# Cross-attention with image prompts: the context transposed by VectorE instead of TensorE, with its load and a few stages around it moved

## The chip, the cores and the metric

The kernel runs on one NeuronCore of a Trainium2 chip, all in fp32. Its engines are TensorE (PE; its weight loads are shown apart as PEld), VectorE (DVE), ScalarE (ACT), GpSimd (POOL) and SyncE (SP), which here only issues DMAs. The metric is the time of one execution on the device in microseconds, the median of several runs. Before the change it was 448.66 us (three runs, 448.07 to 451.15 us).

## The reference

Eight batches (B) of 112 queries with 320 channels attend, with 20 heads of 16 channels, to a context of 375 rows with 512 channels. The last 4 rows of each context are image prompts, the first 371 are text. Cut to what matters:

```python
q    = heads(x @ W_q);  k_t, v_t = heads(text @ W_k), heads(text @ W_v)
p    = softmax(q k_t^T / 4)                       # 112 x 371 per head
text_out = p v_t
qsem = l2norm(p @ text)                           # 112 x 512 per head
sem  = qsem @ l2norm(ip)^T                        # 112 x 4 per head
fused   = q k_ip^T / 4 + 0.5 * sem
probs_ip = softmax(fused) * spatial_mask
out  = (text_out + probs_ip v_ip) @ W_out + b_out + x
```

`p @ text` is never formed. Its norm is the root of p G p with the Gram matrix G = text text^T, and its product with the prompts comes from further columns that stand beside G.

## The kernel before, in words

**Tiling.** A batch has five groups of four heads. For a group, TensorE forms the scores of each head (`scores`, L592, tiles ps_s), VectorE takes the maximum of each row (`probabilities`, L605, nmx), ACT the exponential (L609, p) and a small copy of the prompt logits (L611, ipl), and SP sends p to a tile xg (L614). VectorE turns xg in squares of 32 (`transposed`, L622, xgT, 128 x 1536 elements). Then TensorE multiplies p by the batch's table u, which holds the Gram matrix, the prompts and the values (`multiplied`, L641, ps_qd: twelve steps of four heads side by side). ACT copies the last columns (`value_sums`, L654), and VectorE multiplies the others by p and sums them (`reduced`, L687, one instruction and one accumulator read per head). That frees the four PSUM banks of ps_qd for the next group.

**Between the groups.** After a group's multiplications, `between(b, g)` puts in a piece of other work. In groups 0 to 4 of batch b this is: `gram` of batch b+1 (L415); its `values` (L486); the rest of these and the first piece of its `keys` (L453); the second and third piece of the keys (L453, L444), and queries of later batches (L297, L305); and the transposed context of batch b+2 with further queries. The third piece of the keys is no product but three transposes of columns that were computed with the values. Beside these runs `finish` (called "f") of batch b−1, which joins text and prompts: its weights w (L771, VectorE) are followed on POOL by L827, L838, L839 and L840, which complete the tile attn in group 2 and 3; TensorE turns attn (ps_a, L845) in group 3 and multiplies by W_out (ps_o, L858) in group 4; VectorE adds the bias and residual (L818).

**The transposed context.** A load brings a context into a tile ct, rows on partitions: three DMAs of up to 128 rows of 2 KB and one for seven left-over rows (`load_ctx`, L129, L131). `transposed_context` turns it in three pieces: four TensorE transposes (L357) into one PSUM bank (ps_c) and one copy by ACT (L367) into ctxT, channels on partitions. Gram, values and keys read ctxT. POOL sets ctxT's last columns to zero (L331) and copies the normalised prompts into it (L410). Contexts 0 and 1 are turned in the prologue, the others in the loop.

**What sets the order.** PE, SP and DVE run in the order in which the program writes their instructions, in the main loop ACT too. POOL's order is left to a planner in the loop of the first seven batches, and only in the last batch is it written by hand. All waits come from the tiles' dependences. `run(key, make, pieces)` takes a generator a given number of pieces further. PSUM has eight banks: four for ps_qd, two for scores (`ps_sc`), two for the rest (`ps_mm`); `bank(name, spare=True)` takes one of the two score banks. Both pairs are handed out in turn, so a tile waits for whoever last used its slot. Each DMA queue's completion is counted on one of eight semaphores in turn; a DMA waits for the one issued eight before it.

Of the kernel before, what the change touches and what calls it, by code (L numbers as in the profile page):

```python
# [8 lines left out]
F32 = mybir.dt.float32  # L9
# [11 lines left out]
def kernel(  # L21
# [14 lines left out]
    nc = tc.nc  # L36
    P = 128
    B, S, C = x.shape
    T, E = ehs.shape[1:]
    H = HEADS  # L40
    D = C // H
    TT = T - NIP
    NT = (T + P - 1) // P
    TP = NT * P
    NE = E // P
# [3 lines left out]
    FULL = C // P  # L49
    REST = C - FULL * P  # L50
    RG = 32
# [4 lines left out]
    SCALE = D ** -0.5  # L56
    N = B * NIP

    GROUP = 4
    NG = H // GROUP  # L60
    BLK = TP // RG
    QN = P // RG
# [19 lines left out]
    def bank(name, spare=False):  # L82

        if spare:
            return ps_sc.tile([P, 512], F32, tag="sc", name=name)
        return ps_mm.tile([P, 512], F32, tag="mm", name=name)
# [25 lines left out]
        eng.dma_start(t[:REST, FULL, :C], w[FULL * P :, :])  # L112

    def load_embed(eng, t, w):
        eng.dma_start(t[:, :, :C], w.rearrange("(e p) f -> p e f", p=P))

    def spread(eng, t):

# [2 lines left out]
            eng.tensor_copy(v[:, :, a, 0, :], v[:, :, a // 2, a % 2, :])  # L121
        eng.memset(v[:, :, :, 1, :], 0.0)

    def load_ctx(b):
        ct = io.tile([P, NT, E], F32, tag="ct", name=f"ct_{b}")
        for c in range(NT):
            rows = min(P, T - c * P)
            some = rows - rows % 16
            nc.sync.dma_start(ct[:some, c, :], ehs[b, c * P : c * P + some, :])  # L129
            if some < rows:  # L130
                nc.sync.dma_start(ct[some:rows, c, :], ehs[b, c * P + some : c * P + rows, :])  # L131
        return ct
# [82 lines left out]
    def normalised_prompts():  # L215

        sq = work.tile([N, E], F32, tag="ipn", name="ipsq", bufs=1)
        ss = small.tile([N, 1], F32, tag="ipss", name="ipss", bufs=1)
        nc.vector.tensor_tensor_reduce(
            out=sq, in0=ip_sb, in1=ip_sb, scale=1.0, scalar=0.0, op0=ALU.mult, op1=ALU.add,  # L220
            accum_out=ss,
        )
        nc.vector.tensor_scalar_max(ss, ss, EPS * EPS)
        rn = small.tile([N, 1], F32, tag="iprn", name="iprn", bufs=1)
        nc.scalar.activation(rn, ss, AF.Sqrt)
        nc.vector.reciprocal(rn, rn)

        ipn = work.tile([N, E], F32, tag="ipn", name="ipn", bufs=1)
        nc.vector.tensor_scalar(ipn, ip_sb, rn, 0.5, op0=ALU.mult, op1=ALU.mult)
        yield  # L230

        for src, dst, n in ((ipn, ipnT, "n"), (ip_sb, ipT, "r")):
            ps = bank(f"ps_ipT{n}")
            for e in range(NE):
                nc.tensor.transpose(
                    ps[:, e * N : (e + 1) * N], src[:, e * P : (e + 1) * P], ident[:N, :N]
                )
            nc.vector.tensor_copy(
                dst, ps[:, : NE * N].rearrange("p (e n) -> p e n", n=N)
            )  # L240
        yield
# [82 lines left out]
    def load_next(b):  # L324
        if 2 <= b < B:
            loaded[b] = load_ctx(b)

    def begin(b):
        s = st[b] = dict(ct=loaded.pop(b))
        s["ctxT"] = work.tile([P, NE, TP], F32, tag="ctxT", name=f"ctxT_{b}")  # L330
        nc.gpsimd.memset(s["ctxT"][:, :, T:], 0.0)  # L331

        s["kT"] = work.tile([P, NC, T], F32, tag="kT", name=f"kT_{b}")
        s["vext"] = work.tile([P, NT, C + REST], F32, tag="vext", name=f"vext_{b}", bufs=1)
        s["k3"] = k3
        s["vd"] = dram.tile([TP, C], F32, tag="vd", name=f"vd_{b}")
        s["u"] = work.tile([P, UCOL], F32, tag="u", name=f"u_{b}")
        s["vr"] = work.tile([P, BLK, NG, D], F32, tag="vr", name=f"vr_{b}")
        s["ipl"] = work.tile([S, H, NIP], F32, tag="ipl", name=f"ipl_{b}")
        s["ss"] = work.tile([S, H], F32, tag="ss", name=f"ss_{b}")  # L340
        s["pvs"] = work.tile([S, H, VW], F32, tag="pvs", name=f"pvs_{b}")
        s["vip"] = work.tile([S, NIP, H, D], F32, tag="vipb", name=f"vip_{b}")
# [6 lines left out]
    def transposed_context(b):  # L349
        begin(b)  # L350
        s = st[b]
        ct, ctxT = s["ct"], s["ctxT"]
        for c in range(NT):
            rows = min(P, TT - c * P)
            ps = bank(f"ps_c_{b}_{c}", spare=b > 1 and c > 0)
            for e in range(NE):
                nc.tensor.transpose(  # L357
                    ps[:, e * P : e * P + rows],
                    ct[:rows, c, e * P : (e + 1) * P],
                    ident[:rows, :rows],  # L360
                )
            o = ctxT[:, :, c * P : c * P + rows]
            i = ps.rearrange("p (e t) -> p e t", t=P)[:, :, :rows]
            if c % 2 and b < 1:
                nc.vector.tensor_copy(o, i)
            else:
                nc.scalar.copy(o, i)  # L367
            yield
# [65 lines left out]
    def keys(b):  # L434
        s = st[b]
        if b > 0:
            nc.gpsimd.tensor_copy(s["kT"][:, :, TT:], kip[:, :, b * NIP : (b + 1) * NIP])
        for i in range(NC):
            ps = bank(f"ps_k_{b}_{i}")
            if 0 < b < B - 1 and i == FULL:  # L440

                for c in range(NT):
                    rows = min(P, TT - c * P)
                    nc.tensor.transpose(  # L444
                        ps[:, c * P : c * P + rows],
                        s["k3"][:rows, c].rearrange("p a r d -> p (a r d)"),
                        ident[:rows, :rows],
                    )
                nc.scalar.copy(s["kT"][:, i, :TT], ps[:, :TT])
                yield  # L450
                return
            for e in range(NE):
                nc.tensor.matmul(  # L453
                    ps[:, :TT],
                    wk_sb[:, e, i * P : (i + 1) * P],
                    s["ctxT"][:, e, :TT],
                    start=(e == 0),
                    stop=(e == NE - 1),
                )
            nc.scalar.copy(s["kT"][:, i, :TT], ps[:, :TT])  # L460
            yield
# [16 lines left out]

    def values(b):
        s = st[b]  # L480
        ctxT, vext = s["ctxT"], s["vext"]
        w = C + REST if 0 < b < B - 1 else C
        for c in range(NT):
            ps = bank(f"ps_v_{b}_{c}")
            for e in range(NE):
                nc.tensor.matmul(  # L486
                    ps[:, :w],
                    ctxT[:, e, c * P : (c + 1) * P],
                    wv_sb[:, e, :w],
                    start=(e == 0),  # L490
                    stop=(e == NE - 1),
                )
            nc.scalar.copy(vext[:, c, :w], ps[:, :w])  # L493
            if w > C and c == NT - 1:
                nc.gpsimd.tensor_copy(
                    s["k3"][:, :, :, 0, :],
                    vext[:, :, C:].rearrange("p c (a d) -> p c a d", d=D),
                )
            yield
# [366 lines left out]
            for _ in gen:  # L866
                pass

    LEAD = 2
    steps = [(b, g) for b in range(B) for g in range(NG)]  # L870

    gens = {}
# [1 line left out]
    def run(key, make, pieces=1):  # L874

        if key not in gens:
            gens[key] = make()
        for _ in range(pieces):
            next(gens[key], None)

    def between(b, g):

        nb = b + 1
        new = nb < B
# [21 lines left out]
        if g == 2 and b > 0 and new:  # L906
            run(("f", b - 1), None, 2)
        if g == 3:
            if new:
                run(("k", nb), None, 1)  # L910
            for bs in first if b > 0 else ():
                run(("q", bs[0]), lambda: project_queries(bs), 3)
            if b == 0:
                run(("t", b), lambda: prompt_logits(b))
            if nb < B - 1:
                run(("k", nb), None, 1)
            if b > 0 and new:
                run(("f", b - 1), None)
            for bs in rest:
                run(("q", bs[0]), None)  # L920
        if g == 4:
            if nb + 1 < B:
                run(("c", nb + 1), lambda: transposed_context(nb + 1))
            if b > 0 and new:
                run(("f", b - 1), None, 2)
            if nb + 1 < B:
                run(("c", nb + 1), None, 2)
            for bs in (first if b > 0 else []) + rest:
                run(("q", bs[0]), None)

# [48 lines left out]
    for n, (b, g) in enumerate(steps[:-NG]):  # L979
# [24 lines left out]
        placed(*steps[n + 1])  # L1004
        if g == 0 and b > 1:
            run(("f", b - 2), None)
        if g == 0:
            load_next(b + 2)
        elif g == 1:
            gram_to_groups(b + 1, (1,))  # L1010
        elif g == 3:
            values_to_groups(b + 1)
# [23 lines left out]
    b = B - 1  # L1036
# [126 lines left out]
```

## Time and profile before

| | |
|---|---|
| median of the runs | 448.66 us (448.07 to 451.15) |
| the profiled execution | 449.23 us, span 447.5 us |
| PE busy | 435.1 us, 97% |
| DVE busy | 308.9 us, 69% |
| ACT busy | 196.5 us, 44% |
| POOL busy | 111.1 us, 25% |
| ps_c, PE (L357) | 96 matmuls, median 272 ns, overlapping |
| ctxT copies, ACT (L367) | 23, median 585 ns |
| xgT, DVE (L622) | 40, mean 2976 ns |
| DMA moved | 64.84 MB, mean 145 GB/s |

The profile is of one execution. It gives each instruction's start and duration, and for each idle stretch of an engine what ended it. Matmuls overlap, so the distance between starts says more than the durations. A batch takes about 51.4 us, a group with its piece of other work about 10.3 us.

### The profile page before, as it was taken

The numbers are of one execution on the slowest core, as the hardware profiler recorded it, in microseconds if no ns is written. First come the engines' busy times: TensorE is split into PE (matmuls) and PEld (weight loads), VectorE is DVE, ScalarE is ACT, GpSimd is POOL, SyncE is SP. The second block draws the span as 40 slices with busy tenths as digits, with TensorE's granted clock in tenths as the row PEclk, the third lists the DMA queues.
The fourth block names the chain that finished last, engine by engine and source line by source line (L and its number), as shares of the span: only waits on it lengthen the run. The fifth ranks groups of instructions, "written<-read, shape, count | busy, mean of one in ns | idle before, by whom it ended". The sixth has DMA issues, their size and how long they took to land.

```text
span 447.5 us, 13078 instructions
## 1 busy us (share of the span) xinstructions
PE 435.1 (97%) x5095; PEld 336.3 (75%) x5095; DVE 308.9 (69%) x649; ACT 196.5 (44%) x664; POOL 111.1 (25%) x270
## 2 busy tenths in 40 slices
PE   8998999999999999999999999999999999999885
PEld 8756767888778876788777777778777887787782
DVE  4047356787687767786687866776677867878784
ACT  2254232435345353343535463333534454446782
POOL 4302201011150111511142121511133120527420
PEclk9999999999999999999999999999999999999998
DMA  7669955544645566544646466464556437454400
GB/s 237 174 170 259 212 138 141 141 136 139 171 123 135 145 171 167 128 130 142 167 123 158 117 174 163 129 158 149 141 159 147 137 87 196 123 134 112 136 2 26
DMA packets 52159, 64.84 MB, mean 145 GB/s; under 512 B 18370, under 2 KB 44146, under 8 KB 52098
## 3 DMA queue, kind: packets, MB, share of 16 engines
q1 hardware_dynamic: 51658, 63.45, 53.1%
q8 instruction: 40, 0.66, 0.7%
q10 hardware_dynamic: 440, 0.56, 0.4%
q14 instruction: 21, 0.17, 0.1%
HBM read 19.30 MB, written 5.32 MB: 55 GB/s over the span
## 4 chain that ended last, share of the span: by engine, by line
PE 86%; DVE 4%; ACT 4%; DMA 3%; issue 1%; POOL 1%; SPq 1%; DVEq 0%; POOLq 0%; ACTq 0%
PE ps_qd L641 39%; PE ps_v L486 13%; PE ps_g L415 8%; PE ps_k L453 8%; PE ps_s L592 4%; PE ps_q L305 3%; PE ps_o L858 3%; DMA xg<-p 3%; PE ps_c L357 2%; DVE xgT L622 2%; ACT p L609 2%; PE ps_g L387 1%; DVE junk L687 1%; PE ps_w L374 1%; PE ps_k L469 1%
## 5 line engine op out<-in xcount | busy, mean ns | idle before, releaser
L641 PE MATMUL ps_qd<-u,xgT 32*112 32x104 f32 (+11 forms) x3840 | 217.9, 352 | 3.4 <-DVE xgT L622 1.2
L641 PEld LDWEIGHTS ps_qd<-u,xgT 32*112 32x112 f32 x3840 | 185.8, 172 | 36.7 <-issue 10.3
L605 DVE TENSOR_REDUCE nmx<-ps_s 112x1 f32<-112x371 f32 x160 | 77.6, 529 | 72.4 <-PE ps_s L592 72.3
L622 DVE STREAM_TRANSPOSE xgT<-xg 128x1536 f32<-128x1536 f32 x40 | 119.0, 2976 | 8.0 <-DMA xg<-p 7.4
L609 ACT ACTIVATE p<-ps_s,nmx 112x371 f32<-112x371 f32 x160 | 86.9, 582 | 80.7 <-DVE nmx L605 58.0
L687 DVE CUSTOM_DVE_ANT_0 junk<-ps_qd,p 112x371 f32<-112x371 f32 x148 | 80.2, 542 | 15.8
L559 POOL COPY u<-vr 128x64 f32<-128x64 f32 x120 | 25.8, 236 | 163.9 <-PE ps_qd L641 106.5
L592 PE MATMUL ps_s<-kT,qm 32*112 32x375 f32 (+1 forms) x320 | 64.8, 481 | 0.4 <-ACT p L609 0.4
L486 PE MATMUL ps_v<-wv_sb,ctxT 128*128 128x384 f32 (+1 forms) x192 | 63.5, 480 | 0.0
L486 PEld LDWEIGHTS ps_v<-wv_sb,ctxT 128*128 128x128 f32 x192 | 35.2, 190 | 19.7
L453 PE MATMUL ps_k<-ctxT,wk_sb 128*128 128x371 f32 x136 | 45.9, 482 | 0.0
L654 ACT COPY pvs<-ps_qd 112x21 f32<-112x21 f32 x150 | 16.0, 188 | 64.3 <-PE ps_qd L641 63.4
L415 PE MATMUL ps_g<-ctxT 128*128 128x375 f32 (+2 forms) x168 | 37.4, 379 | 0.0
L453 PEld LDWEIGHTS ps_k<-ctxT,wk_sb 128*128 128x128 f32 x136 | 25.1, 190 | 15.3 <-issue 0.5
L415 PEld LDWEIGHTS ps_g<-ctxT 128*128 128x128 f32 x168 | 28.1, 190 | 8.4
L592 PEld LDWEIGHTS ps_s<-kT,qm 32*112 32x112 f32 x320 | 25.9, 170 | 5.7 <-ACT kT L460 2.1
L314 DVE TENSOR_SCALAR qm<-ps_q,emask 128x224 f32<-128x224 f32 (+1 forms) x25 | 9.2, 400 | 23.6 <-PE ps_q L305 23.6
L611 ACT COPY ipl<-ps_s 112x4 f32<-112x4 f32 x140 | 23.5, 168 | 0.0
L493 ACT COPY vext<-ps_v 128x384 f32<-128x384 f32 (+1 forms) x24 | 11.2, 466 | 25.4 <-PE ps_v L486 25.4
L460 ACT COPY kT<-ps_k 128x371 f32<-128x371 f32 x17 | 8.0, 470 | 25.3 <-PE ps_k L453 25.3
L403 ACT ACTIVATE ug<-ps_g 128x375 f32<-128x375 f32 (+2 forms) x24 | 9.0, 376 | 22.4 <-PE ps_g L415 17.9
L827 POOL TENSOR_TENSOR wv<-vip,w 112x1280 f32<-112x1280 f32 x6 | 14.8, 2461 | 14.6 <-DVE w L771 14.6
(131 smaller groups left out, 336.4 us busy)
## 6 DMA issues: line engine op xcount, KB each, us to landing
xg<-p SPq DMA_DIRECT2D x160, 162.3 KB
u<-ug SPq DMA_DIRECT2D x128, 99.0 KB
ct<-in_ctx_dram SPq DMA_DIRECT2D x16, 256.0 KB
vip<-vipd SPq DMA_DIRECT2D x7, 560.0 KB
vr<-vd SPq DMA_DIRECT2D x32, 120.0 KB
vd<-vext SPq DMA_DIRECT2D x7, 320.0 KB
ct<-in_ctx_dram SPq DMA_DIRECT2D x8, 224.0 KB
vd<-vext SPq DMA_DIRECT2D x7, 160.0 KB
```

What stands on the lines that cost most here:

```text
L415: nc.tensor.matmul(ps[:, : T - t0], ctxT[:, e, t0 : t0 + P], ctxT[:, e, t0:T], start=(e == 0), stop=(e == NE - 1),)
L453: nc.tensor.matmul(ps[:, :TT], wk_sb[:, e, i * P : (i + 1) * P], s["ctxT"][:, e, :TT], start=(e == 0), stop=(e == NE - 1),)
L486: nc.tensor.matmul(ps[:, :w], ctxT[:, e, c * P : (c + 1) * P], wv_sb[:, e, :w], start=(e == 0), stop=(e == NE - 1),)
L559: nc.gpsimd.tensor_copy(region(b, c)[:, :, UV - c * P :], s["vr"][:, c * QN : (c + 1) * QN, g, :])
L592: nc.tensor.matmul(ps[:S, :w], qm[a * RG : (a + 1) * RG, i, r, j * S : (j + 1) * S], s["kT"][a * RG : (a + 1) * RG, i, :w], start=True, st ...
L605: nc.vector.tensor_reduce(nmx, ps[:S, :TT], AX.X, ALU.max, negate=True)
L609: nc.scalar.activation(p, ps[:S, :TT], AF.Exp, bias=nmx)
L611: nc.scalar.copy(s["ipl"][:, groups[g][a], :], ps[:S, TT:T])
L622: nc.vector.transpose(xT.rearrange("p j (k q) -> p q j k", q=QN), xg.rearrange("p q (j k) -> p q j k", k=RG),)
L641: nc.tensor.matmul(banks[a][:S, j * RG : UW], xT[a * RG : (a + 1) * RG, j, :S], region(b, c)[a * RG : (a + 1) * RG, q, q * RG :], start=(j ...
L654: nc.scalar.copy(s["pvs"][:, h, :], ps[:S, TT:UW])
L687: nc.vector.tensor_tensor_reduce(out=junk, in0=ps[:S, :TT], in1=s["p", g][:, a, :], scale=1.0, scalar=0.0, op0=ALU.mult, op1=ALU.add, accu ...
```

## The change

The contexts of batches 2 to 7 are no longer turned by TensorE. Their load puts the rows where VectorE can turn them in squares of 32: row 32j + i of the context is split into four quarters of 128 channels, and quarter a goes to partition 32a + i. This takes four DMAs of 32 partitions x 11 runs of 512 B and four of 19 runs for the last rows, after POOL has zeroed the last 128 columns of the tile; that memset takes the place of the one on ctxT. Channels stand in another order on the partitions: partition p holds channels 4p to 4p+3. So the weights are loaded in that order too (one run of 5 KB per partition instead of four of 1.25 KB), and the transposes of the prologue, of contexts 0 and 1 and the prompts, pick every fourth channel (`chunk`).

`transposed_context` issues three VectorE transposes of 128 x 512 elements for such a context, one at the end of each of groups 0, 1 and 2 (in batch 0: 1, 2 and 3) instead of one stretch in group 4. There is no PSUM bank and no ACT copy in this. The load is issued at the end of group 4 instead of group 0 of the next batch.

In group 3, "f" (ps_a) now comes ahead of the keys and queries instead of behind the keys. The third piece of the keys moves from group 3 to group 4, behind "f" (ps_o), and takes a score bank instead of one of the two others. The tile vext is requested later, at its first use.

```diff
     def load_embed(eng, t, w):
-        eng.dma_start(t[:, :, :C], w.rearrange("(e p) f -> p e f", p=P))
+        eng.dma_start(t[:, :, :C], w.rearrange("(p e) f -> p e f", e=NE))
...
+    def chunk(t, e):
+        return t.rearrange("t (p e) -> t e p", e=NE)[:, e, :]
...
     def load_ctx(b):
         ct = io.tile([P, NT, E], F32, tag="ct", name=f"ct_{b}")
+        if b >= LEAD:
+            v = ct.rearrange("p c e -> p (c e)").rearrange("p (j f) -> p j f", f=P)
+            full = TT // RG
+            nc.gpsimd.memset(v[:, full, :], 0.0)
+            for a in range(QN):
+                nc.sync.dma_start(
+                    v[a * RG : (a + 1) * RG, :full, :],
+                    ehs[b, : full * RG, a * P : (a + 1) * P].rearrange("(j i) f -> i j f", i=RG),
+                )
+            for a in range(QN):
+                nc.sync.dma_start(
+                    v[a * RG : a * RG + TT - full * RG, full, :],
+                    ehs[b, full * RG : TT, a * P : (a + 1) * P],
+                )
+            return v
...
-        nc.gpsimd.memset(s["ctxT"][:, :, T:], 0.0)
+        if b < LEAD:
+            nc.gpsimd.memset(s["ctxT"][:, :, T:], 0.0)
...
     def transposed_context(b):
+        if b >= LEAD:
+            for c in range(NT):
+                some = slice(c * QN, (c + 1) * QN)
+                nc.vector.transpose(
+                    ctxT[:, :, c * P : (c + 1) * P].rearrange("p e (j i) -> p j e i", i=RG),
+                    ct[:, some, :].rearrange("p j (k e) -> p j e k", e=NE),
+                )
+                yield
+            return
         for c in range(NT):
-            ps = bank(f"ps_c_{b}_{c}", spare=b > 1 and c > 0)
+            ps = bank(f"ps_c_{b}_{c}")
             for e in range(NE):
                 nc.tensor.transpose(
...
-                    ct[:rows, c, e * P : (e + 1) * P],
+                    chunk(ct[:, c, :], e)[:rows],
...
     def keys(b):
-            ps = bank(f"ps_k_{b}_{i}")
+            ps = bank(f"ps_k_{b}_{i}", spare=0 < b < B - 1 and i == FULL)
...
     def between(b, g):
         if g == 3:
+            if b > 0 and new:
+                run(("f", b - 1), None)
             if new:
                 run(("k", nb), None, 1)
             for bs in first if b > 0 else ():
                 run(("q", bs[0]), lambda: project_queries(bs), 3)
             if b == 0:
                 run(("t", b), lambda: prompt_logits(b))
+            for bs in rest:
+                run(("q", bs[0]), None)
+        if 0 <= g - (b == 0) < NT and nb + 1 < B:
+            run(("c", nb + 1), lambda: transposed_context(nb + 1))
+        if g == 4:
+            if b > 0 and new:
+                run(("f", b - 1), None, 2)
             if nb < B - 1:
                 run(("k", nb), None, 1)
-            if b > 0 and new:
-                run(("f", b - 1), None)
-            for bs in rest:
-                run(("q", bs[0]), None)
-        if g == 4:
-            if nb + 1 < B:
-                run(("c", nb + 1), lambda: transposed_context(nb + 1))
-            if b > 0 and new:
-                run(("f", b - 1), None, 2)
-            if nb + 1 < B:
-                run(("c", nb + 1), None, 2)
             for bs in (first if b > 0 else []) + rest:
                 run(("q", bs[0]), None)
...
-        if g == 0:
+        if n == 0:
             load_next(b + 2)
-        elif g == 1:
+        if g == NG - 1:
+            load_next(b + 3)
+        if g == 1:
             gram_to_groups(b + 1, (1,))
```

More of the change, by code (lines that the diff above doesn't have):

```diff
@@ L57 @@
     N = B * NIP
+    LEAD = 2
     GROUP = 4
@@ L235, in normalised_prompts @@
                 nc.tensor.transpose(
-                    ps[:, e * N : (e + 1) * N], src[:, e * P : (e + 1) * P], ident[:N, :N]
+                    ps[:, e * N : (e + 1) * N], chunk(src, e), ident[:N, :N]
                 )
@@ L330, in begin @@
         s["ctxT"] = work.tile([P, NE, TP], F32, tag="ctxT", name=f"ctxT_{b}")
-        nc.gpsimd.memset(s["ctxT"][:, :, T:], 0.0)
+        if b < LEAD:
+            nc.gpsimd.memset(s["ctxT"][:, :, T:], 0.0)
         s["kT"] = work.tile([P, NC, T], F32, tag="kT", name=f"kT_{b}")
-        s["vext"] = work.tile([P, NT, C + REST], F32, tag="vext", name=f"vext_{b}", bufs=1)
         s["k3"] = k3
@@ L480, in values @@
         s = st[b]
+        s["vext"] = work.tile([P, NT, C + REST], F32, tag="vext", name=f"vext_{b}", bufs=1)
         ctxT, vext = s["ctxT"], s["vext"]
@@ L867, in drain @@
                 pass
-    LEAD = 2
     steps = [(b, g) for b in range(B) for g in range(NG)]
```

## The prediction

> **What bounds the kernel now.** I read the page's engine shares first, then the chain that ended last, then the windows of one batch's stage, then the timeline of groups 3 and 4 of one batch (batch 3), engine by engine.
>
> ```profile
> PE 435.1 (97%) x5095; PEld 336.3 (75%) x5095; DVE 308.9 (69%) x649; ACT 196.5 (44%) x664; POOL 111.1 (25%) x270
> ...
> PE 86%; DVE 4%; ACT 4%; DMA 3%; issue 1%; POOL 1%; SPq 1%; DVEq 0%; POOLq 0%; ACTq 0%
> ```
> TensorE is busy 97% of the span and is 86% of the chain. The windows of batch 3 say the same (columns: stage, its length, then busy of PE, PEld, DVE, ACT, POOL):
> ```profile
> 203.30:254.50 51.20, 51.13 (x625) 39.23 (x621) 37.64 (x81) 22.90 (x80) 12.57 (x28) 1.00 0.55 147
> ```
> So TensorE has 0.07 us of idle time in 51.2 us. A TensorE instruction removed is time won, and a TensorE wait added is time lost. VectorE has 13.6 us to spare. Now TensorE in groups 3 and 4 (start, duration, line):
> ```profile
> 235.25 2.76 PE L453 MATMUL ps_k<-ctxT,wk_sb 128*128 128x371 f32 x8
> 237.85 0.74 PE L297 MATMUL ps_x<-ident,x_sb 112*128 112x112 f32 x6
> 238.66 0.51 PE L444 MATMUL ps_k<-ident,k 128*128 128x128 f32 x3
> 239.16 0.48 PE L845 MATMUL ps_a<-ident,attn 112*128 112x112 f32 x3
> 239.57 1.22 PE L641 MATMUL ps_qd<-u,xgT 32*112 32x392 f32 x10
> ...
> 244.94 0.66 PE L357 MATMUL ps_c<-ident,ct 128*128 128x128 f32 x4
> 245.43 1.78 PE L858 MATMUL ps_o<-wo_sb,aT 128*112 128x320 f32 x6
> 247.04 0.99 PE L357 MATMUL ps_c<-ident,ct 128*128 128x128 f32 x8
> 247.88 1.31 PE L305 MATMUL ps_q<-xT,wq_sb 128*128 128x224 f32 x6
> 249.12 1.22 PE L641 MATMUL ps_qd<-u,xgT 32*112 32x392 f32 x10
> ```
> See the twelve context transposes (ps_c, L357) in group 4, and that ps_a (L845) is now the last thing before the next group. What ps_a reads is finished on POOL here:
> ```profile
> 230.29 2.46 POOL L827 TENSOR_TENSOR wv<-vip,w 112x1280 f32<-112x1280 f32 x1 [1.91 <-DVE w L771]
> 232.83 1.55 POOL L838 TENSOR_TENSOR wv<-wv 112x640 f32<-112x640 f32 x1
> 234.46 0.86 POOL L839 TENSOR_TENSOR attn<-attn,wv 112x320 f32<-112x320 f32 x1
> 235.41 0.86 POOL L840 TENSOR_TENSOR attn<-attn,wv 112x320 f32<-112x320 f32 x1
> ```
> The last attn ends at 236.27, 2.9 us before TensorE asks for it, but 1.02 us after group 3's matmuls give way (235.25). VectorE, end of group 2, start of group 3, and the last reduction of group 4:
> ```profile
> 229.91 0.30 DVE L771 SCALAR_TENSOR_TENSOR w<-ex,sm_sb,rx 112x80 f32<-112x80 f32 x1
> 231.48 1.00 DVE L605 TENSOR_REDUCE nmx<-ps_s 112x1 f32<-112x371 f32 x2 [1.27 <-PE ps_s L592]
> ...
> 247.82 0.54 DVE L687 CUSTOM_DVE_ANT_0 junk<-ps_qd,p 112x371 f32<-112x371 f32 x1
> ```
>
> **What the Trainium skill says.** "PSUM — Partial Sum Buffer", section "Engine vs sequencer instructions": "MATMULs start and complete in program order". The trace agrees as far as it can: in batch 5 ps_k's transposes (L444) waited 0.17 us for ACT and ps_a stayed behind them. So a ps_a that waits holds up ps_k behind it. "VectorE: DVE Perf Modes", section "The three transpose paths": VectorE transposes 32x32 blocks only and writes SBUF, which is what lets PSUM banks and ACT copies fall away; the trace has xgT (L622), 2976 ns for 1536 elements per partition. "SBUF — State Buffer", section "Specifications (TRN2)": 16-byte lines, and each crossing to a new line pays a penalty. xgT writes with a 16-byte step and takes 1.94 ns per element; no row here reads with such a step, which the new transposes and the strided weight loads of the prologue do.
>
> **The change, part by part.** All sums are for the profiled execution, 449.23 us (span 447.5 us); the median of the runs is 448.66 us, 0.57 below.
>
> *Transposes leave TensorE.* In group 4 of batches 1 to 5, ps_c takes 245.43 − 244.94 = 0.49 us and 247.88 − 247.04 = 0.84 us: 1.33 us. The third keys piece (L444, 0.50 us in odd batches, 0.33 in even ones) moves from group 3 to group 4. Group 4's work between the multiplications is then ps_o 1.61 + ps_k 0.45 + ps_q 1.24 = 3.30 us against 4.18 us. It meets a floor: the last of the four banks is freed when the reduction started at 247.82 ends (0.54 plus its accumulator read 0.08): 248.45, 3.5 us after 244.94. The fourth head comes about 0.1 us after the first, so the stage is worth 3.4 us. Won: 0.78 us. In batch 5 (3.70 us before, only one batch of queries) 0.3 us.
>
> *ps_a goes to the front of group 3.* It waits for POOL, and for the PSUM slot of the score tile of head 0, which ACT leaves at 236.38 (copy L611 at 236.23, 0.15). POOL's order is not written by hand in this stage but planned, and in the built program two instructions come between L827 and L838 in batches 1 to 3: the prompt copy into ctxT (0.20 us, L410) and the memset of the next context tile, 128x128. That memset is bounded by 0.13 us (128x36, L331) and 1.39 us (128x1536, L177); by interpolation 0.2 us. With gaps this delays POOL by 0.45 us; in batches 4 and 5 only the copy stands there, 0.22 us. A semaphore (in group 3 a kT copy of ACT ended at 230.47 and the weight load waiting for it began at 230.51: 0.04 us; I take 0.06) and the first weight load (0.14 us, L845) follow. Stall in batch 3: 236.27 + 0.45 + 0.2 − 235.25 = 1.67 us. The same sum with POOL's end and the group's end of each batch: 1.60 us (batch 1: 133.42, 132.47), 1.67 (batch 2: 184.71, 183.69), 1.48 (batch 4: 287.54, 286.48), 1.65 (batch 6: 389.45, 388.00, nothing inserted). In batch 5 ACT is later than POOL (340.48 against 338.04): 2.5 us, of which 0.55 us comes back, since TensorE waited that long in the next group before. Queued behind ps_a are ps_k, ps_x or ps_q and the next group; who waits for those is ACT and VectorE, both with time to spare.
>
> *Per batch.* Group 3 changes by the stall less the moved keys piece: +1.11, +1.34, +1.17, +1.15. Less 0.78 each: +0.33, +0.56, +0.39, +0.37 for batches 1 to 4. Batch 5: 2.5 − 0.35 − 0.55 − 0.3 = +1.3, of which I take 1.1. Batch 6 loses no transposes, it had none: +1.65. Batch 0 has no ps_a: group 3 gains 0.35; in group 4 (3.37 us before, with a 0.50 us wait for a PSUM slot, which ps_k inherits) the bank floor allows 0.2: −0.55. Sum: +3.85 us.
>
> *Eighteen VectorE transposes.* 512 elements each: 1.0 us at xgT's rate. Bounds: 0.6 us (if xgT's dear part is its writing step and reads with such a step cost nothing) and 2.0 us (if they cost as much again); I take 1.0, the same rate. Behind groups 0 and 1 VectorE idles 2.96 and 3.26 us; behind group 2 from 230.21 to 231.48, 1.27 us. Cost nothing; without that cover each 1 us over would delay scores. Their first piece waits for the load.
>
> *The load.* Eight issues on SP instead of four. At 0.42 us (L129) they hold SP some 3.4 us, from 247.8, after the p transfers of heads 0 and 1 and before vip and the p transfers of heads 2 and 3 (251.9 before), which are needed a group later. It is used at about 257.5, so it has 6 us. Packets are 512 B instead of 2 KB, four times as many; u, vr and p are issued in other groups. Nothing, up to +1 us.
>
> *Prologue.* Weight loads in longer runs: ps_v follows the first gram at once now, so no gain. 24 context transposes and 8 of the prompts read their stationary operand with a 16-byte step. Not faster than dense; at most double (0.14 us each), and only batch 0's twelve lie on the path: 0 to 1.7 us; I take 0.3.
>
> *Bank changes, vext, ctxT's memset.* Off the path: ps_k waits in group 4 for ACT's copy 1.1 us after the group, behind 1.61 us of ps_o. Zero.
>
> Sum: 449.23 + 3.85 + 0.3 = 453.4; for the median **452.9 us**. That is +0.95%, just inside the 1% that about marks what a measurement of this kernel can tell from no change.
>
> **The rivals.**
> (A) As forecast: the stall eats the gain, 450 to 455 us. Chance 0.68. If POOL is not delayed by the inserted pair, the stalls are 1.1 us and it is 450.5.
> (B) No stall: POOL's spans are rough, and if attn is ready when group 3 ends the change keeps all of batches 1 to 5: 1.2 us in each (0.78 and the moved 0.35 to 0.5), batch 0's 0.55 and the prologue's 0.3: 448.66 − 6.0 − 0.55 + 0.3 = 442.4 us for the median. For it: TensorE is the bound and loses work. Against: ACT's slot alone gives 1.1 us. A half-way case gives 446. Chance together 0.14.
> (C) Slower: the transposes on VectorE, at group 2. Above 1.3 us they push the maxima (L605) of the next scores, above 1.8 us ACT's slot comes later than POOL, and ps_a waits longer still. At the upper bound of 2.0 us VectorE is 0.75 us late, ACT's slot 1.1 + 0.75 = 1.85 us and with its semaphore 1.9 us behind the group: 0.25 us more than POOL in five batches, 452.9 + 1.3 = 454.2 us. Against: the new form writes densely, so its rate should not be worse than xgT's. Chance 0.12.
> (D) The load lands late: if it takes over 12 us, VectorE stands at its first piece and the whole group behind it; 1 us each in five batches, 458. Chance 0.06.
>
> Faster by over 1% (below 444.2): 0.08, the pure case of B. Slower by over 1% (above 453.1): the upper part of A (its spread is some 2 us, from the terms above), C and D, 0.42. The rest 0.50. Range 446.5 to 457: near B's half-way case at the bottom; at the top C with the upper bounds of the prologue (1.4 more) and of the load (1 more), 456.6.
>
> **What would show it.** ps_a at the head of group 3 with TensorE idle 1.4 to 1.7 us before it, released by POOL, six times; group 4 shorter by 0.8 us; transposes of 1.0 us with no wait behind them; 0.3 us or less in the first twelve ps_c. Wrong if ps_a starts at once, if a transpose exceeds 1.8 us, or if VectorE waits for ct.

## The result, and the profile after

The changed kernel takes 451.76 us (median; 450.00 to 453.33) against 448.57 us (447.54 to 451.15). The ratio is 1.0073, 95% interval 1.0057 to 1.0089: slower by 0.7%, inside the 1% that the prediction named, and 1.1 us under the time that it gave. The profiled execution took 451.08 us (span 449.3).

The page of the changed kernel first, its engine shares and the chain that ended last:
```profile
PE 427.6 (95%) x5023; PEld 331.1 (74%) x5023; DVE 325.8 (73%) x667; ACT 188.7 (42%) x646; POOL 111.5 (25%) x270
...
PE 64%; DVE 13%; POOL 8%; ACT 4%; DMA 4%; issue 3%; SPq 2%; DVEq 0%; POOLq 0%; ACTq 0%
```
TensorE did lose work (435.1 to 427.6 us), but its share of the chain fell from 86% to 64%, and POOL's rose from 1% to 8%: the end is now set by a chain that runs through other engines. The windows of batch 3 say the same (stage, its length, busy of PE, PEld, DVE, ACT, POOL):
```profile
199.18:250.25 51.07, 49.89 (x610) 38.72 (x609) 40.39 (x84) 21.39 (x77) 12.85 (x29) 1.00 0.62 147
```
The same stretch before the change, from the start of group 0 of batch 3 to that of batch 4 (the prediction's window begins later in group 0):
```profile
197.89:249.12 51.23, 51.16 (x622) 39.25 (x621) 37.31 (x78) 22.90 (x80) 12.84 (x30) 1.00 0.54 147
```
1.27 us less TensorE work than before, but the batch is only 0.16 us shorter: TensorE now idles 1.18 us. The timeline of TensorE, groups 3 and 4 of batch 3, shows where:
```profile
235.74 1.07 PE L673 MATMUL ps_qd<-u,xgT 32*112 32x168 f32 x36
237.99 0.51 PE L877 MATMUL ps_a<-ident,attn 112*128 112x112 f32 x3 [1.18 <-POOL attn L872]
238.33 2.67 PE L484 MATMUL ps_k<-ctxT,wk_sb 128*128 128x371 f32 x8
240.84 0.74 PE L318 MATMUL ps_x<-ident,x_sb 112*128 112x112 f32 x6
...
246.98 1.87 PE L890 MATMUL ps_o<-wo_sb,aT 128*112 128x320 f32 x6
248.69 0.48 PE L475 MATMUL ps_k<-ident,k 128*128 128x128 f32 x3
249.01 1.31 PE L326 MATMUL ps_q<-xT,wq_sb 128*128 128x224 f32 x6
250.25 1.21 PE L673 MATMUL ps_qd<-u,xgT 32*112 32x392 f32 x9
```
ps_a stands first and waits, and ps_k behind it waits with it. Group 4's other work has shrunk from 4.18 us to 250.25 − 246.98 = 3.27 us. POOL's timeline in the same place:
```profile
231.79 2.47 POOL L859 TENSOR_TENSOR wv<-vip,w 112x1280 f32<-112x1280 f32 x1 [1.92 <-DVE w L803]
234.20 0.20 POOL L441 COPY ctxT<-ipnT 128x16 f32<-128x16 f32 x1
234.33 0.20 POOL L135 MEMSET ct<- 128x128 f32 x1
234.49 1.56 POOL L870 TENSOR_TENSOR wv<-wv 112x640 f32<-112x640 f32 x1
236.13 0.87 POOL L871 TENSOR_TENSOR attn<-attn,wv 112x320 f32<-112x320 f32 x1
237.08 0.86 POOL L872 TENSOR_TENSOR attn<-attn,wv 112x320 f32<-112x320 f32 x1
```
The last attn ends at 237.94 and ps_a begins at 237.99. ACT's copy of the logits of head 0, whose end frees the score bank that ps_a takes, is hardly earlier:
```profile
237.71 0.15 ACT L643 COPY ipl<-ps_s 112x4 f32<-112x4 f32 x1
```
It ends at 237.86. The query of the context's transposes on VectorE (count, then min/median/max in ns), and of the wait ahead of ps_a over the whole execution:
```profile
L378 DVE STREAM_TRANSPOSE ctxT<-ct x18: 1089/1102/1118, 62.4 to 334.1; 128x512 f32<-128x512 f32 x18
```
```profile
its engine sat idle before it (us, times) until:
  POOL attn L872: 5.3, 4
  POOL u L591: 3.3, 2
```
Eighteen transposes of 1.1 us, none waiting for ct, and 8.6 us of idle TensorE in front of ps_a in six batches. Two of the six, in batches 4 and 5, bear the name of the POOL copy that follows attn. By the ends of the instructions it was ACT's copy of head 0 that came last there, at 288.83 and 341.33 us, 0.10 us before ps_a began; in batch 1 too it came last, by 0.03 us.

Stage by stage, from the starts of the groups' first ps_qd matmuls, after minus before in us:

| batch | group 3 | group 4 and the next group 0 | stall ahead of ps_a |
|---|---|---|---|
| 0 | −0.32 | −0.41 + 0.60 | none |
| 1 | +0.42 | −0.82 + 0.12 | 1.17 |
| 2 | +1.06 | −0.91 + 0.19 | 1.56 |
| 3 | +0.46 | −0.81 + 0.10 | 1.18 |
| 4 | +0.62 | −0.92 + 0.22 | 1.15 |
| 5 | +1.24 | −1.41 + 0.57 | 2.18 |
| 6 | +1.46 | 0.0 | 1.44 |
| sum | +4.94 | −3.48 | 8.68 |

Three stretches are left: the prologue −0.15, group 0 of batch 0 +1.70 and the last batch about −1.2. The last two come from TensorE's clock, which the last section takes up. Without them the stages sum to −0.15 + 4.94 − 3.48 = +1.3 us.

### The profile page after: what moved, and what is told of

The parts are those of the page before. It is cut to its first block, busy times and chain, and to the rows that moved or that the text cites. A ratio compares the mean times of both kernels' runs of the same rounds, so it can differ in the third digit from the quotient of the medians.

```text
span 449.3 us, 12963 instructions
## 1 busy us (share of the span) xinstructions
PE 427.6 (95%) x5023; PEld 331.1 (74%) x5023; DVE 325.8 (73%) x667; ACT 188.7 (42%) x646; POOL 111.5 (25%) x270
## 4 chain that ended last, share of the span: by engine, by line
PE 64%; DVE 13%; POOL 8%; ACT 4%; DMA 4%; issue 3%; SPq 2%; DVEq 0%; POOLq 0%; ACTq 0%
PE ps_qd L673 27%; PE ps_g L446 8%; PE ps_v L518 7%; PE ps_k L484 6%; DVE xgT L654 4%; PE ps_s L624 3%; DVE junk L719 3%; PE ps_q L326 3%; PE ps_o L890 2%; DMA u<-ug 2%; POOL wv L859 2%; DVE nmx L637 2%; POOL wv L870 2%; SPq L646 1%; PE ps_g L418 1%
## 5 line engine op out<-in xcount | busy, mean ns | idle before, releaser
L624 PE MATMUL ps_s<-kT,qm 32*112 32x375 f32 (+1 forms) x320 | 66.6, 484 | 0.4 <-ACT p L641 0.4
L624 PEld LDWEIGHTS ps_s<-kT,qm 32*112 32x112 f32 x320 | 26.8, 170 | 6.7 <-ACT kT L491 2.1
L378 DVE STREAM_TRANSPOSE ctxT<-ct 128x512 f32<-128x512 f32 x18 | 19.8, 1103 | 0.0
L859 POOL TENSOR_TENSOR wv<-vip,w 112x1280 f32<-112x1280 f32 x6 | 14.8, 2467 | 15.0 <-DVE w L803 15.0
```

The source lines that it names most:

```text
L624: nc.tensor.matmul(ps[:S, :w], qm[a * RG : (a + 1) * RG, i, r, j * S : (j + 1) * S], s["kT"][a * RG : (a + 1) * RG, i, :w], start=True, st ...
L859: eng.tensor_tensor(wv, s["vip"][:, :, part], w.rearrange("p h n -> p n h").unsqueeze(3).to_broadcast([S, NIP, n, D]), ALU.mult,)
```

## The experiments

Each run has its own median; the kernel before had 448.0 to 448.2 us beside them, so that they may be compared with each other and with 451.8 us. Stage figures are of the profiled executions. Three of these lie well below their median: in run 3 (444.3 us against 446.5), run 6 (453.84 against 456.39) and run 10 (443.26 against 445.74).

**1. Only ps_a put back behind the queries** (changed kernel otherwise).
```diff
         if g == 3:
-            if b > 0 and new:
-                run(("f", b - 1), None)
             if new:
                 run(("k", nb), None, 1)
...
                 run(("t", b), lambda: prompt_logits(b))
+            if b > 0 and new:
+                run(("f", b - 1), None)
```


> Only the place of ps_a in group 3 goes back: behind the keys and the queries of the pair, all else as in the changed kernel. Theory A (the stall at ps_a eats the gain): the stalls of the changed kernel, 7.0 us in its trace, go; 451.8 - 7.0 = 444.8 us, 443 to 446, and PE waits less than 0.3 us in all before ps_a. Rival C (VectorE's new work holds the groups up): the wait only changes its place, 450 us or more. Rival 'the floor of the ps_qd banks': with group 3 shorter, the floor moves to group 3 as well and half of it stays, 447 to 449.

Measured: 445.6 us, ratio to the kernel before 0.994 (0.9922 to 0.9958). The edit of one place turns the change from 0.7% slower into 0.6% faster; theory A holds. (The stalls that it takes away sum to 8.68 us, not to the 7.0 us of the expectation.) The waits did not all go: in odd batches ps_a now waits 0.5 to 0.6 us, 1.6 us in all where less than 0.3 was expected, for ACT's copies of ps_x, since it takes a score bank that ps_x has used. Batch 3:
```profile
236.80 0.74 PE L318 MATMUL ps_x<-ident,x_sb 112*128 112x112 f32 x6
238.11 0.48 PE L877 MATMUL ps_a<-ident,attn 112*128 112x112 f32 x3 [0.57 <-ACT xT L321]
```
So group 3 is 0.5 us shorter than before in batches 2 and 4, and equal to it in 1 and 3.

**2. Only ps_a first, in the kernel before.**
```diff
         if g == 3:
+            if b > 0 and new:
+                run(("f", b - 1), None)
             if new:
...
                 run(("k", nb), None, 1)
-            if b > 0 and new:
-                run(("f", b - 1), None)
```


> The kernel before with ps_a alone moved to the front of group 3; the context is still turned by TensorE. Theory A: the stall comes without any of the other edits, 1.0 to 1.3 us in batches 1 to 4, about 2 in batch 5 and 1.4 in batch 6: 448.6 + 7 = 455.5 us, 454 to 457. Rival C (it is VectorE's new work that makes ps_a late): below 450 us.

Measured: 456.0 us, ratio 1.0174 (1.0147 to 1.0202). The stall is there without any VectorE transpose; with the first run this leaves the place of ps_a as its cause.

**3. Only the transposes, load and weights.** ps_a and the third keys piece stand where they stood before.
```diff
-            ps = bank(f"ps_k_{b}_{i}", spare=0 < b < B - 1 and i == FULL)
+            ps = bank(f"ps_k_{b}_{i}")
...
         if g == 3:
-            if b > 0 and new:
-                run(("f", b - 1), None)
...
+            if nb < B - 1:
+                run(("k", nb), None, 1)
+            if b > 0 and new:
+                run(("f", b - 1), None)
...
         if g == 4:
...
-            if nb < B - 1:
-                run(("k", nb), None, 1)
```


> The context turned by VectorE, with its load and its weights, and ps_a and the third piece of the keys where they were before, in the banks of before. Theory A: group 4 falls to the floor of the banks, 0.8 us less in batches 1 to 4 and 0.3 in batches 0 and 5, and nothing else changes: 448.6 - 3.7 + 0.3 (prologue) = 445.2 us, 444 to 446.5, slower than the kernel with only ps_a put back by about 1 to 2 us because the keys piece stays in group 3. Rival C: 448.6 us or more. Rival 'no floor': group 4 falls by 1.33 us, 442.5 us.

Measured: 446.5 us, ratio 0.995 (0.993 to 0.997), at the upper edge of what was expected. It is 0.9 us slower than run 1 by the medians, but the two intervals overlap and the profiled executions stand the other way about, so that difference is not shown. What the run shows is the floor of the banks at work. Group 4 of batches 1 to 4 falls by 1.25 us, almost the whole 1.33 us of TensorE work, but group 0 behind it grows by 0.52 to 0.69 us, as TensorE stands before the fourth head's bank. Timeline of TensorE there:
```profile
195.81 1.22 PE L673 MATMUL ps_qd<-u,xgT 32*112 32x392 f32 x9
196.57 0.47 PE L624 MATMUL ps_s<-kT,qm 32*112 32x375 f32 x1
196.79 0.54 PE L673 MATMUL ps_qd<-u,xgT 32*112 32x392 f32 x3
```
The group starts, but with three heads only (these rows are merged): the fourth head's first multiplication begins at 196.37, where in the kernel before all four began within 0.02 us. Its bank is freed by VectorE's fourth reduction, which ends at 196.30:
```profile
195.76 0.54 DVE L719 CUSTOM_DVE_ANT_0 junk<-ps_qd,p 112x371 f32<-112x371 f32 x1
```
Group 4 of batch 1 and group 0 of batch 2 together take 8.30 + 11.16 = 19.46 us here, 8.63 + 10.83 = 19.46 us in run 1, against 9.55 + 10.63 = 20.18 us before: 0.72 us won, whether the keys piece is in group 4 or not. That is why the piece can move there for nothing.

**4. Every context transpose twice** (18 x 1.1 us more on VectorE).
```diff
                 nc.vector.transpose(
                     ctxT[:, :, c * P : (c + 1) * P].rearrange("p e (j i) -> p j e i", i=RG),
                     ct[:, some, :].rearrange("p j (k e) -> p j e k", e=NE),
                 )
+                nc.vector.transpose(
+                    ctxT[:, :, c * P : (c + 1) * P].rearrange("p e (j i) -> p j e i", i=RG),
+                    ct[:, some, :].rearrange("p j (k e) -> p j e k", e=NE),
+                )
```


> The changed kernel with each of the 18 context transposes issued twice on VectorE, 18 x 1.1 us more on that engine. Theory A: behind groups 0 and 1 VectorE has the time; behind group 2 only 0.22 us are left, so the maxima of group 3 come 0.9 us late, but POOL still ends later than ACT's copy; 451.8 to 452.8 us. Rival C (VectorE's time at these places sets the end): 0.9 us in each of six batches, 456 us or more.

Measured: 457.36 us, ratio 1.0223 (1.0192 to 1.0253): +5.6 us on the changed kernel, where theory A had at most 1. The expectation failed. VectorE's timeline behind group 2 of batch 3 (group 3 starts at 232.63):
```profile
232.92 1.11 DVE L378 STREAM_TRANSPOSE ctxT<-ct 128x512 f32<-128x512 f32 x1
234.06 1.11 DVE L382 STREAM_TRANSPOSE ctxT<-ct 128x512 f32<-128x512 f32 x1
235.09 0.96 DVE L641 TENSOR_REDUCE nmx<-ps_s 112x1 f32<-112x371 f32 x2
235.96 2.98 DVE L658 STREAM_TRANSPOSE xgT<-xg 128x1536 f32<-128x1536 f32 x1
238.80 0.92 DVE L641 TENSOR_REDUCE nmx<-ps_s 112x1 f32<-112x371 f32 x2
```
The first maxima begin 2.46 us after group 3's start instead of 1.59. Of this I had counted only the later end of ACT's copies ahead of ps_a. But the next scores stand within the group's multiplications and need the banks that ACT frees, so TensorE waits already there: the multiplications end 6.12 us after the start instead of 5.44, and ps_a begins 7.40 us after it instead of 6.62. Not all of the 5.6 us is VectorE's. This profile has two stretches of low TensorE clock (last section), in group 3 of batches 3 and 5, and the six executions had a mean clock of 0.990 against 0.996 for the changed kernel. From that I estimate 2.5 us for the clock and some 3 us for the transposes. By the stages of the two profiles, without the clock's part, it is 4.6 us.

**5 and 6. Doubling a part.** To see whether VectorE's load or the place costs, the first two transposes of a batch were doubled in one run, the third alone in the other.
```diff
+                for _ in range(2 if c < 2 else 1):
-                nc.vector.transpose(
+                    nc.vector.transpose(
...
```
(In the second run `c == 2` in place of `c < 2`.)

> The changed kernel with only the first and second context transpose of each batch issued twice. Theory 'the third piece's place': behind groups 0 and 1 VectorE has over 1.5 us to spare, so 451.8 us and at most 1 us more from batch 0, whose second piece lies behind group 2; below 453 us. Rival 'VectorE's whole load': two thirds of the 5.6 us of doubling all, 455.5 us.

> The changed kernel with only the third context transpose of each batch issued twice (behind group 2, in batch 0 behind group 3). Theory 'the third piece's place': nearly all of the 5.6 us of doubling all comes back here, as 1.1 us more than the 0.22 us left ahead of the maxima of group 3: 455 to 457 us. Rival 'VectorE's whole load': one third, 453.6 us.

Measured: 453.0 us (ratio 1.010, 1.0072 to 1.0128) and 456.39 us (1.0188, 1.0161 to 1.0215): +1.2 and +4.6 us. It is the place. The 1.2 us are just about what batch 0 lost, whose second piece lies behind group 2 (its group 3 took 1.13 us more); batch 5 shows another 1.0 us in that profile. There VectorE waited 2.06 us for p to land ahead of group 3's xgT, against 0.97 us in the changed kernel, and ACT's copy and ps_a came later by as much; whether the doubling made that transfer late is not shown. With the first two pieces doubled, groups 0 to 2 of batches 1 to 5 take the same time as in the changed kernel to 0.02 us, and group 3 of batches 2 and 3 changes by −0.39 and +0.35. With the third doubled, group 3 grows by 0.35 to 0.80 us in each of batches 1 to 4, and group 4 of batch 0 by 1.12 us, 3.6 us in all by the stages. That is less than the 4.6 us of the medians, and the mean clock of these six executions was lower too, 0.994.

**7, 8 and 9. Which wait holds ps_a?** In one run the two last additions on POOL are left out, in one ps_a is given an ordinary bank, in the third both.
```diff
-            eng.tensor_tensor(ah, ah, wv[:, 0], ALU.add)
-            eng.tensor_tensor(ah, ah, wv[:, 1], ALU.add)
...
-        ps = bank(f"ps_a_{b}_{h0}", spare=not late)
+        ps = bank(f"ps_a_{b}_{h0}")
```


> The changed kernel without the two last additions on POOL: the weighted prompt values are not added to attn, so the output lacks the prompts' part; ps_a no longer waits for this chain. In the trace of the changed kernel ACT's copy of the prompt logits of head 0, which frees the score bank that ps_a takes, ends within 0.1 us of POOL's last addition in batches 1, 3 and 4, 0.4 us before it in 2 and 6, and 1.1 us after it in 5. Theory 'two waits of equal length': only 0.8 us comes back, 451.8 - 0.8 = 451.0 us, and the wait is still there under ACT's name. Theory 'POOL alone', as the forecast has it for all batches but 5: the stall goes in all but batch 5, 446 to 447 us.

> The changed kernel with ps_a in one of the two ordinary banks instead of a score bank; POOL's chain as it is. Theory 'two waits of equal length': batch 5 gains 1.1 us, the others 0.1 us at most, 450.6 us, and the wait stays with POOL. Theory 'the score bank alone': the stall goes, 445 to 446 us. Theory 'POOL alone': only batch 5's part, 450.6 us too.

> Both at once: no last additions on POOL (the prompts' part of the output is missing) and ps_a in an ordinary bank. Theory 'two waits of equal length': now the whole 7 to 8 us stall goes, 443.5 to 445 us, though ps_a still stands at the head of group 3. If the place at the head costs something of its own, the queue behind it for one, it stays above 447 us.

Measured: 450.93 us (ratio 1.0061, 1.0040 to 1.0083), 449.58 us (1.0025, 1.0013 to 1.0038) and 445.09 us (0.9932, 0.9907 to 0.9957). The wait ahead of ps_a, first without the additions, then with the other bank:
```profile
  ACT ipl L643: 8.0, 6
```
```profile
  POOL attn L872: 7.3, 6
```
Take one away and the other stands there with nearly the same length; take both and it is gone. The two removals are worth 0.8 and 2.2 us alone and 6.7 us together. Of the 2.2 us some 1.3 are an estimate for the clock, whose mean was 0.999 there against 0.996 in the changed kernel; that leaves about the 1.1 us that were expected from batch 5. The page names only the later of two waits, and in the changed kernel's trace the earlier one ends 0.03 to 0.42 us before the later in five of the six batches. Standing first costs nothing in itself: the third run is as fast as the first experiment.

**10. ps_a between keys and queries.**
```diff
         if g == 3:
-            if b > 0 and new:
-                run(("f", b - 1), None)
             if new:
                 run(("k", nb), None, 1)
+            if b > 0 and new:
+                run(("f", b - 1), None)
```


> The changed kernel with ps_a behind the second piece of the keys (2.7 us of matmuls) and ahead of the queries. Both waits end 1.2 us (batch 5: 2.1 us) after the group, so the keys cover them. Theory A: as with ps_a put back behind the queries, and without the 0.5 us that ps_a then waited for ACT's copies of ps_x in batches 1, 3 and 5: 445.6 - 1.5 = 444.1 us, 443 to 445. Rival: the keys' copy or ps_x takes over the 0.5 us, 445.6 us.

Measured: 445.74 us, ratio 0.9936 (0.9914 to 0.9957): no better than behind the queries. The profiled execution is the fastest of the six, so what the slower ones lost it need not show. Group 3 of batches 1 and 3 did become 0.34 us shorter than before, but then group 4 of batch 3 met another wait. VectorE's timeline there:
```profile
237.84 0.99 DVE L637 TENSOR_REDUCE nmx<-ps_s 112x1 f32<-112x371 f32 x2 [2.08 <-PE ps_s L624]
239.63 2.96 DVE L654 STREAM_TRANSPOSE xgT<-xg 128x1536 f32<-128x1536 f32 x1 [0.80 <-DMA xg<-p]
```
and SP's queue before it:
```profile
229.69 1.78 SPq L646 DMA_DIRECT2D xg<-p  x2
231.52 3.87 SPq L460 DMA_DIRECT2D u<-ug  x4
235.49 1.84 SPq L646 DMA_DIRECT2D xg<-p  x2
```
Four transfers of the next batch's table hold the second pair of p on the queue until 235.49. With a longer group 3 there was time for that.

**11. The same, with those four transfers behind p.**
```diff
-                if 1 <= g <= 3:
-                    gram_to_groups(b + 1, {1: (0,), 2: (2,), 3: (3,)}[g])
+                if 1 <= g <= 2:
+                    gram_to_groups(b + 1, {1: (0,), 2: (2,)}[g])
...
         elif g == 3:
+            gram_to_groups(b + 1, (3,))
             values_to_groups(b + 1)
```


> As the kernel with ps_a between keys and queries, and besides the four transfers u<-ug of group 3 behind the second pair of p transfers on SP's queue instead of ahead of it. In that kernel's trace they hold the queue 3.9 us, the second pair goes out 2 us after its exponentials, and VectorE then waits 0.8 us for p at the turn of group 4's xgT (batch 3), which comes back as a late bank of ps_qd in the next group. Theory 'SP's queue has become the limit of the shorter group 3': groups 4 and 0 together fall from 20.3 to 19.5 us in batches 3 and 4; 445.7 - 1.5 = 444.2 us. Rival (only VectorE's own work is the limit there): 445.7 us.

Measured: 444.91 us, ratio 0.9922 (0.9897 to 0.9948), the lowest of all, though its interval overlaps those of runs 1 and 10 and its profiled execution, 445.26 us, was slower than that of run 10. What is shown is the gain at the two places that the edit aimed at, not one in the whole. The queue in the same group:
```profile
230.22 5.40 SPq L646 DMA_DIRECT2D xg<-p  x4
235.67 2.49 SPq L460 DMA_DIRECT2D u<-ug  x4
238.21 2.16 SPq L543 DMA_DIRECT2D vr<-vd  x4
```
Groups 4 and 0 fall back to 8.63 + 10.83 = 19.46 us in batches 3 and 4, as expected (they had 20.34 and 20.01 in run 10). Batch 5 lost 0.7 us on the kernel before in that profile, with p landing late again while other transfers were under way; this I did not pursue. The version beats both kernels: its median is 0.8% below the kernel before, and 1.5% below the change as it was made.

## Why the prediction was right

The likeliest case, a stall at ps_a that eats the gain, is what happened: 451.76 us against 452.9. By its own steps:

- **Transposes leave TensorE, down to a floor** (0.78 us a batch, 0.3 in batch 5 and 0.2 in batch 0; −3.6 us in all). The sum came out, −3.48 us, in part by errors that cancel: batches 1 to 4 won 0.70 to 0.72 us each. The floor is real, but it doesn't show where I put it. Group 4 itself may fall below it (by 1.25 us in experiment 3), and the rest is paid in the next group 0, inside the multiplications. In batch 0 nothing was won (−0.41 and +0.60, a loss of 0.2 where a gain of 0.2 stood), in batch 5 0.84 us instead of 0.3.
- **ps_a at the front waits** (stalls of 1.60, 1.67, 1.67, 1.48, 2.5 and 1.65 us, 10.6 in all). Right in kind, too large: 8.68 us. Two terms were mis-sized. The first is what POOL's planner puts ahead of L870. I gave it 0.45 us in batches 1 to 3, from durations and gaps. In batch 3 L870 starts at 234.49, where L859 ends at 234.26: 0.23 us, against the gap of 0.08 us that the same two instructions had before; the pair costs 0.15 us. That is −0.3 us in each of the three batches; the copy alone, priced at 0.22 us, cost nothing in batch 4 (a gap of 0.08 again). The second is the 0.2 us for the semaphore and the first weight load: ps_a began 0.05 us after the last attn in batch 3, and 0.10 us after ACT's copy in batches 1, 4 and 5. In batch 2 an unforeseen wait hid this: in its reductions of group 2 VectorE stood 0.50 us, by the profile for an ACT copy (vext), so that w, and POOL behind it, came 0.4 us later.
- **What releases ps_a.** The prediction named both POOL and ACT's score bank, and put POOL clearly later after the delay. With the delay small, the two are nearly equal, and ACT came last in batches 1, 4 and 5. So "released by POOL six times" holds for the labels alone: experiments 7 to 9 show that taking POOL away was worth 0.8 us. In batch 5 the prediction itself has ACT last. (Its "340.48 against 338.04" sets ACT against the end of the group's multiplications. POOL ended there at 339.04, and the 2.5 us stand.)
- **Group 3** (+7.7 us in all with the moved keys piece). Measured +4.94: 1.9 us of the difference is the stall, the rest is about 0.2 us in each of batches 1 to 4, by which the group shrank beyond the keys piece.
- **VectorE's transposes** (1.0 us, free). 1.1 us and free, but by a hair: the idle time ahead of group 3's maxima fell from 1.27 to 0.22 us. Rival C was the right mechanism at a wrong price: 1.3 us at 2.0 us per transpose, where experiment 4 has 3 to 5.6 us at 2.2 us (by how much the clock is counted), because I priced only ACT's bank ahead of ps_a and not the scores within the group.
- **The load** (free). Right: SP issues it for 3.4 us as computed, and no transpose waited for it. Nothing in these runs prices the smaller packets.
- **The prologue** (0.3 us). Its strided weight loads take 210 ns against 140, as the bounds allowed, but the first group started at 36.52 us against 36.67. Starts of 35.8 to 37.6 us among the profiles of these runs hide anything of that size.
- **Rival B** (no stall, 442.4 us) is what experiments 1, 9 and 10 built: 445.1 to 445.7 us. It was 3 us too good, as it gave all five batches 1.2 us; the waits for ps_x's banks, for SP's queue and at batch 5 take a part.

By profile the sum is −0.15 + 1.70 + 4.94 − 3.48 − 1.2 = +1.8 us of span. The medians differ by 3.2 us, because the profiled execution before was 0.66 us above its median and that after 0.68 us below. That the prediction came within 1.2 us was in part luck: by the profiles alone (453.4 against 451.08) it was 2.3 us too high, and the stages that it priced sum to +1.3 us where it had 3.85 + 0.3 = 4.15. (453.38 less 0.57 is 452.8, not 452.9; it changes nothing.) What fills the gap in part is the clock, of which the prediction said nothing.

In the Trainium skill, "PSUM — Partial Sum Buffer", section "Engine vs sequencer instructions", the in-order rule of matmuls was the base of the argument, and the trace agrees: ps_k, whose data were ready, started 0.34 us after ps_a in the timeline above and never before it.

## What to carry to other kernels

Before moving an instruction to the head of an in-order queue, list every operand and every buffer slot that it needs and when each comes free; two waits that end together must both be removed before much is won, and the profile names only one, not always the right one. Work taken off the bounding engine pays only down to the next release (here a PSUM bank), and a shorter stage turns a queue order that used to be harmless into a wait. An engine with 27% idle time can have 0.2 us of slack at the one place that matters: look at the idle time ahead of the instruction that would be delayed, not at the share.

## What the runs showed of the hardware that was not expected

**TensorE's clock drops to half for some 3.4 us**, in the profiles of several of these kernels, at changing places. Windows of the changed kernel in batch 0 (the clock is third from the end):
```profile
50.00:52.00 2.00, 2.00 (x5) 0.71 (x4) 0.23 (x1) 0.05 (x1) 1.95 (x7) 0.50 1.03 177
52.00:54.00 2.00, 2.00 (x8) 0.64 (x10) 0.00 (x0) 0.18 (x1) 0.00 (x0) 0.66 1.18 199
```
and of the kernel before in its last batch:
```profile
440.00:442.00 2.00, 1.87 (x5) 0.99 (x5) 1.40 (x4) 0.08 (x1) 0.00 (x0) 0.66 0.00 0
442.00:444.00 2.00, 1.60 (x4) 0.45 (x2) 0.00 (x0) 0.25 (x1) 0.00 (x0) 0.50 0.23 72
```
In the first place it costs 1.70 us, the whole growth of batch 0's group 0; in the second it lies in the last batch, which in the changed kernel's profile has no such stretch and is some 1.2 us shorter. The profile of experiment 1 has no such stretch and that of experiment 4 has two, at 240 and 346 us. Comparing two single profiles without a look at the clock would have found causes in the code for both.

It bears on the medians too. One such stretch lowers the mean clock of an execution to 0.996. The changed kernel had 0.996 or less in 9 of 10 executions, the kernel before in 15 of the 52 beside the experiments, experiments 4 and 6 in all 12, experiment 8 in 1 of 22. At 1.7 us each, I estimate that about 1 us of the 3.2 us between the medians is the clock's; how much of it belongs to the change is not shown. The finding on ps_a does not hang on this: experiments 1, 2 and 9 moved the time by 6 us and more.

What sets it off is open. Work missing on TensorE just before does not decide it: the stretch at 50 us follows 6.8 us in which TensorE never idled, and none follows the 3.4 us from 183.04 us in the changed kernel, in which it was busy for 1.86 us only.

**Short operations on POOL cost less than they last.** By the records the copy and the memset last 0.20 us each and overlap: they and the next operation start 0.13 and 0.16 us apart. Between the two operations around them they added 0.15 us together.

**VectorE's transposes.** 512 elements per partition in squares of 32 take 1102 ns, 2.15 ns per element, with a read at a 16-byte step and a dense write; xgT, which writes at such a step, takes 1.94 ns. TensorE's weight load of 128 x 128 fp32 took 210 ns with that step (ps_c after) and 140 ns dense (ps_c before).
